# A graph network on one core: the attention targets' a_dst by a broadcast DMA from DRAM, and the gathered slots' lane at every pair of blocks

## The chip, the cores and the metric

The kernel runs on one core of a Trainium2 chip. The core has a matrix engine (TensorE; PE for its matmuls, PEld for the loads of its stationary operand), VectorE (DVE), ScalarE (ACT), GpSimd (POOL) and SyncE (SP), which here only issues DMAs. Sixteen DMA engines serve all queues. The metric is the device time of one execution in microseconds (us); less is better.

## The reference

Four graph layers follow each other over the same 6250 nodes with 128 features and the same 206250 edges, sorted by target. After each layer its result is added to x and normalised. The change touches the end of the third layer and the fourth, a graph attention with 4 heads of 32 channels:

```python
h = (x @ W).reshape(N, H, C)
a_src = jnp.sum(h * att_src, axis=-1)
a_dst = jnp.sum(h * att_dst, axis=-1)
logits = a_src[src] + a_dst[dst]
logits = jnp.where(logits > 0, logits, NEG_SLOPE * logits)
seg_max = jax.ops.segment_max(logits, dst, num_segments=N)
e = jnp.exp(logits - seg_max[dst])
denom = jax.ops.segment_sum(e, dst, num_segments=N)
alpha = e / (denom[dst] + EPS)
msgs = h[src] * alpha[:, :, None]
out = jax.ops.segment_sum(msgs, dst, num_segments=N)
```

So a_dst is one number for each node and head: 25000 numbers in all.

## The kernel before

Nodes lie in 49 blocks of 128, the last of 106. Layer 0 builds a dense adjacency (how often each source meets each target, in bf16) and stores it in DRAM as `adj`; layer 1 works on edges; layers 2 and 3 stream `adj` back. The program order is written out by hand: each engine, and SP's queue of DMAs, takes its instructions in that order.

**Layer 2 (`dense2`).** It goes over 25 targets' stretches of 256 nodes, two blocks each (below also called a block, counted from 0). `add(sb, ...)` first issues the loads of that stretch's adjacency on SP (L1061: four tiles of 11 source blocks, 704 KB each, and one of 5), then runs 3 x 49 matmuls (L822), and after every ten of them takes a step or two of `node2` for an earlier stretch. The first three stretches begin early, and up to stretch 6 two steps are taken each time, one afterwards. `A11` has six buffers, so the loads of the next stretch can start while this one is being summed. At a stretch's end ACT takes the sum out (L1078).

**`node2`** computes the new x, `h` and the attention terms: `al[:, 0]` holds a_src and `al[:, 1]` a_dst, one column for each block and head, with the node on the partition. For each of the two a product (L531) and a reduce (L533) run on DVE. Then two stores go out on SP (L537): h and a_src, into `t3`, which the gather of layer 3 reads. The loads of a later stretch stand behind those stores in SP's queue.

**Layer 3 (`attend`).** 48 target blocks are summed densely: six groups of 1024 targets times four heads give 24 units (counted from 0), each with 25 pairs of source blocks. For a pair, SP loads 512 KB of adjacency (L1390, four DMAs, three pairs ahead, four buffers), ACT makes a mask `r` from a_dst along the free axis and a_src as the bias (L1423, twice), DVE forms `B` and `C` (L1429, L1431), and PE runs ten matmuls of 512 columns (L1444). The pairs' loop ends with one step of each of four lanes:

- `sums`: `close` of the unit before, then `targets` of the next unit. A step is due two pairs after the last.
- `news`: the tables of the next head (ACT casts at L1239, DVE subtractions at L1241). The first head's tables are made inside unit 0.
- `ends`: the final normalisation of finished groups.
- `others`: `gathered`, the last block of 106 targets. It takes the block's sources by gathers on POOL (64 of 128 rows each), in eight chunks of eight slots: three adds on DVE, an exp on ACT (L1342), a product on DVE (L1345) and 16 matmuls into a sum on PE (L1348; each float32 product counts as two). Gathers run three chunks ahead, with four buffers.

**`targets`** brings a_dst of a unit's 1024 targets onto all partitions, as the free axis of a tile `ad`: for each of its eight blocks PE transposes the column of `al`, broadcast over 128 columns (L1259), into one PSUM bank, and ACT copies each four of them to SBUF (L1256, L1264).

Of the kernel before, what the change touches and what calls it, by code (L numbers as in the profile page):

```python
# [9 lines left out]
F32 = mybir.dt.float32  # L10
# [8 lines left out]
P = 128  # L19
# [4 lines left out]
F = 512  # L24
D = 128
HEADS = 4
# [42 lines left out]
def kernel(  # L69
# [9 lines left out]
    nc = tc.nc  # L79
    N = x.shape[0]  # L80
# [27 lines left out]
    dram = ctx.enter_context(tc.tile_pool(name="dram", bufs=1, space=bass.MemoryType.DRAM))  # L108
# [15 lines left out]
    R0 = rest[0][0] // P if rest else NB  # L124
    slot_src = dram.tile([max(2, 2 * NS - R0 // 2 * 2), P, S], I32)
    slot_not = dram.tile([max(2, 2 * NS - R0 // 2 * 2), P, S], F32)
    t3d = dram.tile([N + W, 2 * HEADS], F32)
    adj = dram.tile([NS, P, NB * 2 * P], BF16)
    ea_rows = edge_attr.rearrange("(r t) d -> r (t d)", t=T)

    def store(table, t, n0, rows, nb, eng=nc.sync):
        eng.dma_start(table[n0 : n0 + rows * nb].rearrange("(b p) d -> p b d", p=rows), t[:rows, :nb, :])
# [11 lines left out]
    ident = const.tile([P, P], F32)  # L144
# [201 lines left out]
    def transposed(pool, pps, t, rows, nb, name, G=4):  # L346

        pt = pps.tile([P, F], F32, name="na")
        for b in range(nb):
            nc.tensor.transpose(pt[:, b * rows : (b + 1) * rows], t[:rows, b, :], ident[:rows, :rows])  # L350
        yield
        r = pool.tile([P, G * P], F32, name=name)
        nc.scalar.copy(r[:, : rows * nb], pt[:, : rows * nb])
        yield
        return r
# [19 lines left out]
    def update(pool, po, n0, rows, nb, plus=None, G=4):  # L375

        xb = xn[:, n0 // P : n0 // P + nb, :]
        t = pool.tile([P, G, D], F32, name="res")
        nc.vector.tensor_add(t[:rows, :nb], po[:rows, :nb], (xb if plus is None else plus)[:rows, :nb])
        yield from layernorm(pool, t, xb, rows, nb)  # L380
        return xb
# [120 lines left out]
    def node2(acc, al, pool, pps, n0, rows, nb, G=4, hT=None):  # L502

        n = rows * nb
        b0 = n0 // P
        keep = hT is not None
        if not keep:
            hT = pool.tile([P, G * P], F32, name="hT")
            nc.scalar.activation(hT[:, :n], acc[:, 0, n0 : n0 + n], AF.Relu, bias=c1c)
        m = pool.tile([P, G, D], F32, name="m")  # L510
        nc.gpsimd.tensor_add(m[:rows, :nb], xn[:rows, b0 : b0 + nb, :], c2b[:rows].unsqueeze(1).to_broadcast([rows, nb, D]))
        yield
        po = pps.tile([P, 4, D], F32, name="na")
        for b in range(nb):
            nc.tensor.matmul(po[:rows, b, :], hT[:, b * rows : (b + 1) * rows], V2s, start=True, stop=True)
        yield
        xb = yield from update(pool, po, n0, rows, nb, m, G)
        xT = yield from transposed(pool, pps, xb, rows, nb, "xT", G)
        ph = pps.tile([P, 4, D], F32, name="na")
        for b in range(nb):  # L520
            nc.tensor.matmul(ph[:rows, b, :], xT[:, b * rows : (b + 1) * rows], Wgs, start=True, stop=True)
        yield
        if keep:
            hs = acc[:, 0, n0 : n0 + nb * D].rearrange("p (b d) -> p b d", d=D)
        else:
            hs = pool.tile([P, G, HW], F32, name="hs")
        nc.scalar.copy(hs[:rows, :nb, :D], ph[:rows, :nb])
        yield
        for k in range(2):
            pr = pool.tile([P, G, D], F32, name="pr")  # L530
            nc.vector.tensor_mul(pr[:rows, :nb], hs[:rows, :nb, :D],  # L531
                                 att[:rows, k : k + 1, :].to_broadcast([rows, nb, D]))
            nc.vector.tensor_reduce(al[:rows, k, b0 : b0 + nb, :],  # L533
                                    pr[:rows, :nb].rearrange("p b (h c) -> p b h c", h=HEADS), AX.X, ALU.add)
        if keep:
            for c, of in ((slice(0, D), hs), (slice(D, HW), al[:, 0, b0 : b0 + nb, :])):
                nc.sync.dma_start(t3[n0 : n0 + n, c].rearrange("(b p) d -> p b d", p=rows), of[:rows, :nb])  # L537
        else:
            nc.vector.tensor_copy(hs[:rows, :nb, D:], al[:rows, 0, b0 : b0 + nb, :])
            store(t3, hs, n0, rows, nb)  # L540
# [103 lines left out]
    def general():  # L644
        with ExitStack() as st:
# [113 lines left out]
            al = gp.tile([P, 2, NB, HEADS], F32, name="al")  # L759
            nc.vector.memset(al, 0.0)  # L760
            nodes("g2", lambda *a: node2(acc, al, *a))
            with tc.tile_pool(name="g3o", bufs=1) as one, tc.tile_pool(name="g3op", bufs=2, space=PSUM) as pps:
                drain(shift3(acc, al, one, one, pps))
# [4 lines left out]
    def fast():  # L768
# [401 lines left out]
        def attend(acc, al):  # L1170
# [9 lines left out]
            for k in range(2):  # L1180
                of = flat[:, k * US : (k + 1) * US].rearrange("p (n k c) -> p n k c", k=3, c=CH + 1)
                tabs.append((of[:, : 2 * NB].rearrange("p (b s) k c -> p b s k c", s=2), of[:, 2 * NB :]))
            units = [(groups[2 * k][0], groups[2 * k : 2 * k + 2]) for k in range(UNITS)]
            with tc.tile_pool(name="f3c", bufs=1) as one, tc.tile_pool(name="f3", bufs=2) as ep, \
# [62 lines left out]
                def width(of):  # L1247
                    return sum(rows * nb for n0, rows, nb in of)

                def targets(k, h, n0, of):  # L1250

                    to = one.tile([P, 2 * F], F32, name=f"ad{k % 2}")
                    last = None
                    for m0, rows, nb in of:
                        if last is not None:
                            nc.scalar.copy(*last)  # L1256
                        pt = pps.tile([P, F], F32, name="na")
                        for j in range(nb):
                            nc.tensor.transpose(pt[:, j * rows : (j + 1) * rows],  # L1259
                                                al[:rows, 1, m0 // P + j, h : h + 1].to_broadcast([rows, P]),  # L1260
                                                ident[:rows, :rows])
                        last = (to[:, m0 - n0 : m0 - n0 + rows * nb], pt[:, : rows * nb])
                        yield
                    nc.scalar.copy(*last)  # L1264
                    ready[k] = to

                def close(h, of, s):
# [122 lines left out]
                            nc.sync.dma_start(A[i][:, k, :n].rearrange("p l q -> p (l q)"),  # L1390
                                              adj[sb + k, :, a * 2 * P : (a + n) * 2 * P])

                sums, news, ends, others = Lane(), Lane(), Lane(), Lane(3)
                for i in range(3):
                    load(i)
                drain(targets(0, *steps[0]))
                first = [tables(0, groups[k::2]) for k in range(2)]
                others.add(gathered())
                made, i, now = 0, 0, 0
                for k, (h, n0, of) in enumerate(steps):  # L1400
# [6 lines left out]
                    if k + 1 < len(steps):  # L1407
                        sums.add(targets(k + 1, *steps[k + 1]))
# [49 lines left out]
        with tc.tile_pool(name="facc", bufs=1) as one:  # L1458
            acc = one.tile([P, 3, NA], F32, name="acc")
            for k in range(3):  # L1460
                nc.vector.memset(acc[:, k, :], 0.0)

            two, third = [acc[:, k, 0 : NB * D].bitcast(BF16).rearrange("p (b k d) -> p k b d", k=2, d=D) for k in (1, 2)]
            parts = [two[:, 0], two[:, 1], third[:, 0]]
            al = one.tile([P, 2, NB, HEADS], F32, name="al")
            nc.vector.memset(al, 0.0)
            with tc.tile_pool(name="f1n", bufs=1) as pool, tc.tile_pool(name="f1np", bufs=2, space=PSUM) as pps:
                left = mlp("f1", lambda *a: node1(acc, parts, *a), pool, pps)
                dense2(parts, lambda *a: node2(acc, al, *a), left)
            attend(acc, al)  # L1470
# [40 lines left out]
```

## Time and profile before

| | us |
|---|---|
| median of 18 runs (5471.37 to 5515.95) | 5495.12 |
| the profiled execution | 5501.77 |
| its span | 5500.0 |
| layer 2's last sum ends | 3888 |
| attention's pairs (first B to last) | 3910.7 to 5447 |
| PE busy, share of the span | 91% |
| DVE, ACT, POOL busy | 55%, 47%, 36% |

The profile is one execution. In the lines below a row of the timeline has start, duration, engine, line of the program, operation, output and inputs, a count, and in brackets the idle time before it with what ended it. "SPq" is SP's queue: the time is that of issuing, not of the transfer. In a row of stretches each engine has its busy time and number of instructions; a matmul's record is modelled, so neighbouring ones can overlap a little. PEclk is the clock granted to TensorE, 1.00 at most. Names of tensors are cut to letters: `t` is t3, `acc` here also holds h.

### The profile page before, as it was taken

To read this page: it belongs to the slowest core of one execution; us is meant where nothing else is said; L and a number is where in the kernel's file an instruction comes from. 1 tells how busy PE (TensorE), PEld (TensorE's weight loads), DVE (VectorE), ACT (ScalarE), POOL (GpSimd) and SP (SyncE) were. 2 spreads that over 40 slices of the span, in tenths; PEclk is the share of its full clock that TensorE was granted. 3 is DMA by queue.
4 is the path that set the end of the run, shared out by engine and by line. 5 is a ranking of instruction groups with operands and counts; after the bars stand their busy time and mean duration, and the time that the engine had idled before them with its cause. 6 is when DMAs were issued, how large, how long until landed. Compare 5 with 4: busy or idle time off the path is not lost.

```text
span 5500.0 us, 90840 instructions
## 1 busy us (share of the span) xinstructions
PE 4991.0 (91%) x33477; PEld 4101.3 (75%) x33477; DVE 3026.8 (55%) x5156; ACT 2569.3 (47%) x3618; POOL 1969.7 (36%) x1926
## 2 busy tenths in 40 slices
PE   4999997889899998998998999999689999999995
PEld 3999997788888887887888888899455555555553
DVE  6887863233333333332333333222578888888998
ACT  3444442222333332332332323100478999999885
POOL 3333425665666666656666566000220000000000
PEclk9999998998998998989998889999899999999998
DMA  5333324444444444444444443455476777777774
GB/s 115 120 134 130 144 108 136 126 124 123 128 127 127 127 130 122 127 120 126 123 126 124 118 123 109 169 196 196 144 176 193 220 215 211 221 215 218 211 212 125
DMA packets 624753, 830.17 MB, mean 151 GB/s; under 512 B 150523, under 2 KB 508449, under 8 KB 620077
## 3 DMA queue, kind: packets, MB, share of 16 engines
q1 hardware_dynamic: 536189, 595.08, 35.0%
q0 software_dynamic: 87120, 228.54, 14.6%
q8 instruction: 268, 4.39, 0.3%
q14 instruction: 184, 1.51, 0.1%
q10 hardware_dynamic: 992, 0.66, 0.0%
HBM read 730.60 MB, written 93.31 MB: 150 GB/s over the span
## 4 chain that ended last, share of the span: by engine, by line
PE 35%; ACT 7%; DVE 5%; DMA 2%; issue 2%; SPq 1%; another core or an unknown queue 1%; DVEq 0%; POOL 0%; ACTq 0%; POOLq 0%
PE s L1444 12%; PE sum L822 7%; PE seg L1143 6%; ACT r L1423 6%; PE pre L1129 5%; DVE B L1429 2%; DMA A<-adj 2%; PE na L1282 1%; PE tp L1118 1%; SPq L1390 1%; DVE sT L1275 0%; ACT acc L1239 0%; PE na L456 0%; DVE C L1431 0%
## 5 line engine op out<-in xcount | busy, mean ns | idle before, releaser
L135 POOL DMA_INDIRECT g<-t,edges x1617 | 1584.4, 980 | 1004.1 <-issue 762.8
L1423 ACT ACTIVATE r<-ad,bias 128x1024 bf16<-128x1024 f32 x1176 | 1254.1, 1139 | 107.0 <-DVE B L1429 104.7
L1131 DVE TENSOR_TENSOR g<-g,pre 128x512 f32<-128x512 f32 x882 | 548.7, 641 | 1304.9 <-PE pre L1129 416.6
L1444 PEld LDWEIGHTS <-acc 128*99 128x99 bf16 x5856 | 737.6, 127 | 663.9 <-issue 172.0
L1143 PE MATMUL seg<-oh,g 128*128 128x64 f32 (+1 forms) x6468 | 1036.6, 284 | 50.2 <-issue 47.2
L1143 PEld LDWEIGHTS seg<-oh,g 128*128 128x128 f32 (+1 forms) x6468 | 959.7, 205 | 93.0 <-issue 59.1
L1129 PE MATMUL pre<-W1s,eaT 128*128 128x256 f32 (+1 forms) x3234 | 908.0, 423 | 113.1 <-DVE g L1131 64.1
L1444 PE MATMUL s<-B,acc 128*99 128x512 bf16 x3504 | 874.6, 384 | 111.7 <-DVE B L1429 97.5
L1132 ACT ACTIVATE g<-g 128x512 f32<-128x512 f32 x882 | 505.8, 592 | 764.4 <-DVE g L1131 528.9
L1129 PEld LDWEIGHTS pre<-W1s,eaT 128*128 128x128 f32 (+1 forms) x3234 | 644.5, 212 | 246.7 <-issue 111.4
L1429 DVE TENSOR_TENSOR B<-A,r 128x2048 bf16<-128x2048 bf16 x600 | 720.6, 1201 | 137.2 <-ACT r L1423 71.3
L1120 ACT COPY eaT<-tp 128x512 f32<-128x512 f32 (+1 forms) x441 | 240.3, 545 | 1021.1 <-PE tp L1118 295.5
L1143 PE MATMUL seg<-oh,ea 128*128 128x64 f32 (+1 forms) x3234 | 664.2, 287 | 33.4 <-issue 33.0
L1143 PEld LDWEIGHTS seg<-oh,ea 128*128 128x128 f32 (+1 forms) x3234 | 526.6, 204 | 36.9 <-issue 36.8
L939 ACT CAST A<-pa 128x784 bf16<-128x784 f32 x400 | 324.4, 811 | 350.6 <-PE pa L936 323.3
L822 PE MATMUL sum<-A,xs 128*128 128x256 bf16 (+1 forms) x3675 | 471.0, 275 | 0.4 <-ACT A L939 0.4
L1431 DVE TENSOR_TENSOR C<-A,B 128x1024 bf16<-128x1024 bf16 x600 | 415.4, 692 | 68.0 <-PE s L1444 3.6
L822 PE MATMUL sum<-A,acc 128*128 128x256 bf16 (+1 forms) x3675 | 409.5, 271 | 4.4 <-DMA A<-adj 4.4
L822 PEld LDWEIGHTS <-acc 128*128 128x128 bf16 x3675 | 355.2, 98 | 46.2 <-issue 6.1
L822 PEld LDWEIGHTS <-xs 128*128 128x128 bf16 x3675 | 358.8, 102 | 36.8 <-issue 0.6
L936 PE MATMUL pa<-oh,oh 128*128 128x98 bf16 x3200 | 355.8, 268 | 26.9 <-ACT A L939 22.3
L1444 PE MATMUL s<-C,acc 128*99 128x512 bf16 x1200 | 360.2, 382 | 0.3 <-DVE C L1431 0.2
(242 smaller groups left out, 4099.7 us busy)
## 6 DMA issues: line engine op xcount, KB each, us to landing
A<-adj SPq DMA_DIRECT2D x2304, 128.0 KB
ea<-in_edge_attr_dram SPq DMA_DIRECT2D x292, 256.0 KB
A<-adj SPq DMA_DIRECT2D x100, 704.0 KB
ea<-in_edge_attr_dram SPq DMA_DIRECT2D x146, 192.0 KB
g<-t,edges POOLq DMA_INDIRECT x1617
A<-adj SPq DMA_DIRECT2D x25, 320.0 KB
t<-y SPq DMA_DIRECT2D x24, 256.0 KB
A<-adj SPq DMA_DIRECT2D x96, 64.0 KB
```

The lines of the kernel that those rows point to most:

```text
L135: nc.gpsimd.indirect_dma_start(out=to, out_offset=None, in_=table, in_offset=bass.IndirectOffsetOnAxis(ap=index[:K, t : t + 1], axis=0))
L822: nc.tensor.matmul(ps[:, :n], parts[part][:, b, :], a(b)[:, :n], start=k == 0, stop=k == 3 * NB - 1)
L936: nc.tensor.matmul(ps[:, o, q * LO : (q + 1) * LO], ohs[g][0][:, 2 * j + o, :, q], ohs[g][1][:, 2 * j + o, :, q], start=True, stop=True)
L939: nc.scalar.copy(A[sb][:, :, q0 : q0 + 2 * QI].rearrange("p k (o q) -> p k o q", q=QI), ps[:, :, : QI * LO].rearrange("p o (q k) -> p k o ...
L1129: nc.tensor.matmul(pre[:K, t, :], eaT[i][:, b + t, :K], W1s[:, 1, :], start=True, stop=True)
L1131: nc.vector.tensor_add(gb, gb, pre[:K, :n, :])
L1132: nc.scalar.activation(gb, gb, AF.Relu)
L1143: nc.tensor.matmul(ps[:, m, :], rows, oh[c][:K, a + t, :], start=a + t == 0 and m == 0, stop=a + t == T - 1, skip_group_check=True)
L1423: nc.scalar.activation(r[:, l, :n], ad[:, :n], AF.Relu, bias=bias[:, b + l, h : h + 1], scale=BIG)
L1429: nc.vector.tensor_tensor(wide(bt), At[:, :ns, :kk, :w], wide(r), ALU.min)
L1431: nc.vector.tensor_sub(ct[:, :n].rearrange("p (s q) -> p s q", q=w), At[:, :ns, 0, :w], bt[:, 0, :n].rearrange("p (s q) -> p s q", q=w))
L1444: nc.tensor.matmul(s[to][g][:M, : c1 - c0], row, rhs(c0, c1), start=to not in begun, stop=stop)
```

## The change

Layer 2 also writes a_dst to a DRAM tile with a row for each head: for each block one DMA from `al`, an element of 4 bytes for each node and head, issued on SP ahead of the two t3 stores. `targets` becomes one DMA on SP that reads 1024 numbers of a row and writes them to all 128 partitions; its transposes and copies go. It has one step in the `sums` lane where it had three. And `others` is due at every pair where it was due at every third.

```diff
+    a_dst = dram.tile([HEADS, N], F32)
...
         if keep:
+            with nc.allow_non_contiguous_dma(reason="one element a node and head"):
+                for b in range(nb):
+                    nc.sync.dma_start(a_dst[:, n0 + b * rows : n0 + (b + 1) * rows].rearrange("h p -> p h"),
+                                      al[:rows, 1, b0 + b, :])
             for c, of in ((slice(0, D), hs), (slice(D, HW), al[:, 0, b0 : b0 + nb, :])):
...
                     to = one.tile([P, 2 * F], F32, name=f"ad{k % 2}")
-                    last = None
-                    for m0, rows, nb in of:
-                        if last is not None:
-                            nc.scalar.copy(*last)
-                        pt = pps.tile([P, F], F32, name="na")
-                        for j in range(nb):
-                            nc.tensor.transpose(pt[:, j * rows : (j + 1) * rows],
-                                                al[:rows, 1, m0 // P + j, h : h + 1].to_broadcast([rows, P]),
-                                                ident[:rows, :rows])
-                        last = (to[:, m0 - n0 : m0 - n0 + rows * nb], pt[:, : rows * nb])
-                        yield
-                    nc.scalar.copy(*last)
+                    nc.sync.dma_start(to[:, : width(of)], a_dst[h, n0 : n0 + width(of)].partition_broadcast(P))
+                    yield
                     ready[k] = to
...
-                sums, news, ends, others = Lane(), Lane(), Lane(), Lane(3)
+                sums, news, ends, others = Lane(), Lane(), Lane(), Lane(1)
```

## The prediction

> **What bounds the kernel now.** I read the busy time of each engine in stretches first, the timeline of one block of layer 2 next, then the waits of the attention stage and the transfers' packets.
>
> Busy times by stretch (span, then PE, PEld, DVE, ACT, POOL in us with counts, granted clock, DMA share, GB/s): a block of layer 2, then, from a second answer, attention units 0, 1, 2, then 5 to 18, then 19 to 22.
>
> ```profile
> 3724.00:3741.00 17.00, 17.00 (x158) 15.36 (x156) 3.59 (x12) 1.35 (x5) 0.72 (x1) 1.00 0.53 191
> ```
> ```profile
> 3910.70:4010.00 99.30, 71.08 (x270) 39.55 (x271) 61.50 (x106) 65.91 (x84) 37.39 (x34) 0.81 0.49 139
> 4010.00:4084.30 74.30, 63.55 (x316) 39.43 (x316) 57.12 (x85) 57.83 (x65) 19.58 (x19) 0.98 0.78 188
> 4084.30:4163.50 79.20, 68.43 (x315) 41.16 (x315) 56.71 (x83) 56.16 (x62) 9.79 (x9) 0.89 0.71 174
> ...
> 4290.90:5124.60 833.70, 810.61 (x3976) 490.11 (x3974) 729.16 (x970) 772.79 (x823) 0.00 (x0) 1.00 0.72 217
> 5124.60:5377.80 253.20, 233.95 (x1141) 140.54 (x1140) 237.40 (x407) 221.29 (x230) 0.00 (x0) 1.00 0.70 211
> ```
> Layer 2 is PE without a gap. A steady attention unit lasts 833.7/14 = 59.6 us, with PE busy 57.9 and ACT 55.2. Units 19 to 22 lean on DVE too (94%). Units 0 to 2 are 15 to 40 us longer, and PE is not what fills them.
>
> How little lead layer 2 has, from its timeline (start, us, engine, line): block 15 first, then the end of block 3.
>
> ```profile
> 3733.99 0.37 SPq L537 DMA_DIRECT2D t<-acc  x1
> ...
> 3734.91 0.37 SPq L537 DMA_DIRECT2D t<-al  x1
> ...
> 3735.37 2.87 SPq L1061 DMA_DIRECT2D A<-adj  x5
> 3735.37 0.42 DVE L533 TENSOR_REDUCE al<-pr 128x8 f32<-128x256 f32 x1
> 3740.91 0.47 ACT L1078 ACTIVATE hT<-sum,c1c 128x256 f32<-128x256 f32 x1 [6.94 <-PE sum L822]
> ```
> ```profile
> 3528.88 2.71 SPq L1061 DMA_DIRECT2D A<-adj  x5
> ...
> 3532.28 0.47 ACT L1078 ACTIVATE hT<-sum,c1c 128x256 f32<-128x256 f32 x1 [4.76 <-PE sum L822]
> 3533.54 1.25 PE L822 MATMUL sum<-A,acc 128*128 128x256 bf16 x10 [1.29 <-DMA A<-adj]
> ```
> The loads of the next block stand on SP behind the stores of this one's node work. At block 4 they left at 3528.88 and PE began on them at 3533.54: 4.66 us from issue to use, and PE stood 1.29 us. In a steady block they leave 3735.37 and are wanted when the sum before is done, 3740.91 (less 0.03): a lead of 5.51. The slack is 0.85 us. By the packets' own times the first tile lands 1.57 us before that end on average, which gives 0.6. I take 0.7.
>
> Waits of the attention stage (who, on whom: us, times, longest), units 4 to 18, then units 1 and 2; and the transfers during one gather:
>
> ```profile
> DVE B L1429 <- ACT r L1423: 49.3, 53, 2.2
> ...
> ACT ad L1256 <- PE na L1259: 29.5, 15, 2.1
> ```
> ```profile
> DVE B L1429 <- DMA A<-adj: 25.5, 11, 3.7
> ```
> ```profile
> q1 hardware_dynamic: 4171, 3.80, 53.5%
> q0 software_dynamic: 256, 0.54, 33.1%
> ```
> ACT stands about 2 us in each unit for the transposes that carry a_dst. In units 1 and 2 the wait for adjacency tiles is 25.5 us, and in the 24 us window over one chunk of slots the gather (q0) holds a third of the DMA engines.
>
> **The change, part by part.**
>
> *Transposes and copies go.* Per unit 8 transposes (four take 0.43 us on PE, from 4497.63 to the next matmul at 4498.06: 0.87 a unit) and two ACT copies (14.03 + 13.81 us in 24 units: 1.16 a unit), with the 2 us wait ahead of the first. What that is worth depends on who bounds. PE alone gives 0.87 a unit. PE has 833.7 - 810.6 = 23 us idle in 14 units, 1.65 each, so a unit can give 2.5 at most. I take 1.3 for units 3 to 18 (PE-bound ones give 0.87, those in which the next head's tables are made and ACT is full give more), 21 us; 0.9 in the other seven, 6 us; and 1 us of copies ahead of the first r. Sum -28; bounds -14 (DVE-bound and early units give nothing) and -48.
>
> *A broadcast of 512 KB a unit comes.* 24 DMAs on SP, each 128 packets of 4 KB. Packets of 4096 bytes took 0.16 us in stage 1, so 1.3 us of all 16 engines, at pair 9 of 25, right behind a load and ahead of the next. Steady tiles land 1 to 2.5 us before B needs them, so the next load is late by about 1 us and nothing stands; the target row is wanted 15 pairs later. On SP the issue is 0.43 us where four loads of 0.43 fill 1.9 of a pair's 2.4 us. I take +2; bounds 0 and +12 (0.5 us a unit).
>
> *The first broadcast* waits for all of layer 2's a_dst writes and stands behind 12 tile loads on SP (3893.8 to 3899.4); landed about 3905, before the first r at 3908.5, which waits for tables. Zero; if the last block's 424 writes are slow, +3.
>
> *Stores of a_dst come into layer 2.* 49 DMAs of 512 elements of 4 bytes, two for each pair of blocks, ahead of the t3 stores and waiting for the second reduce of al, which ends at 3735.79. Today the t3 stores fit into the wait for DVE; then they queue behind it. SP's order is then: 3735.82 two stores at 0.46 (512-element stores of the output issue in 0.37 to 0.43), then two t3 stores at 0.46, then the loads at 3737.66: 2.3 us later than 3735.37. DVE, ACT and PE get no new work; what is queued behind SP is only the loads, and PE waits for those. Less the slack, 2.3 - 0.7 = 1.6 us a block for blocks 8 to 24 (17 blocks, all with the same lead to 0.6 us): 27 us. Block 4 has no slack: 2.3. Blocks 5 to 7 have 9.9 us of lead: nothing. Sum +29.5.
>
> The price of 4-byte writes into DRAM is in no row. The nearest is the t3<-al store, 16 bytes each: one DMA's 256 packets, in a window that also holds 16 others:
>
> ```profile
> DMA packets 272, 0.00 MB, mean 7 GB/s; under 512 B 272, under 2 KB 272, under 8 KB 272
> ```
> It fits into 0.23 us, so 512 would take 0.46, no longer than SP needs to issue one, and nothing is added. Four times that (3.7 us for two) would put the loads behind a backlog and the delay at 4.75: +70 us in all. Bounds for the part +20 (slack 0.85 and issues of 0.37) and +70; I stay with the row, which is the same queue, store and place.
>
> [...]
>
> *The lane of the gathered slots steps at every pair, not every third.* Chunks 4 to 7 of the gather now start at pairs 24, 36, 48 and 60 (POOL at 4002, 4038, 4073, 4114) and would start at 14, 18, 22 and 26. So three fall into unit 0, where B needs a tile 5 to 7 us after it lands (packet times; in units 1 and 2 it is 1 to 4). Three quarters of the 25.5 us go: -19. PE's sums (16 matmuls, 1.8 us a chunk): five chunks leave units 2 to 4, three come into unit 1, two go into unit 0's idle PE: -3.5. Unit 0 gets two more chunks of DVE work (1.22 + 3 x 0.19 = 1.8 each): +3.6. ACT's exp now comes one pair after DVE's adds (0.57 us) and can stand about 0.5 each, eight times: +4. On POOL a chunk's eight gathers take 10 us (1.25 each) where four pairs of unit 0 last 16, so the data, wanted 12 pairs after its issue, is not late, and POOL has nothing else queued; the two slot loads on SP stay where they are. Sum -15; bounds -26 (every wait gone, no cost) and +8 (waits only moved).
>
> **Sum:** 29.5 - 28 - 15 + 2 = -11.5 us. The profiled execution took 5501.8 us (span 5500.0), 6.7 above the median of 5495.1. Set against the median: 5484.
>
> **The rivals.** *Layer 2 pays more* (ends slower). The 4-byte writes drain slower than 16-byte ones, or SP takes 0.97 us to issue one, as it did for the 550 single elements at the start. [...] Against: the 16-byte row. Each microsecond of delay costs 18 us, so it is even at 2.9 us and slower by 0.2% from 3.5; at 4 us the time is 5495 - 11.5 + 31 = 5515. *The lane moves its waits, not ends them:* for it, that gathers 0 to 3 already cost unit 0 waits; against it, unit 0's spare lead. Part +4 in place of -15: 5503. *The delay in layer 2 is hidden*, because landing and use overlap better than block 4 shows: two blocks that landed 1.03 us ahead ran on within 0.06 us. Then -41: 5454.
>
> The clock gate: PE's 1.29 us wait at block 4 left the granted clock at 1.00. [...]
>
> **How the numbers follow.** The sum as worked 0.45 (alone 5462 to 5507: about half faster by over 0.2%, a third within); layer 2 pays more 0.30 (nearly all slower); the lane's waits stay 0.13 (half slower, half within); hidden 0.12 (faster). 0.2%, 11 us, is what a measurement here can tell. Faster 0.37, within 0.20, slower 0.43. Cases of both signs weigh alike, so the range goes from the hidden case to beyond the first rival's 4 us: 5452 to 5525.
>
> **What would show it.** PE sum waiting for the adjacency DMA in layer 2, about 18 times for some 30 us, with blocks of 18.8 us in place of 17.2. SP's loads 2.3 us later against the end of the sum. The 29.5 us wait of ACT gone, and steady units of 58.3. Units 1 and 2 together 15 to 20 us shorter, unit 0 up to 8 longer. Wrong if layer 2's wait is 60 us or none, or if B comes to wait for tiles at pair 12 or 13 of each unit.

## The result

The changed kernel takes 5917.73 us (median of 10 runs, 5912.39 to 5930.81) where the kernel before takes 5493.25 (median of 62): 1.0774 times as long, 95% interval 1.0757 to 1.0791, or 424 us more. The forecast was 5484 us with a range of 5452 to 5525. It missed by far: the time lies 393 us above the range.

### The profile page after: what moved, and what is told of

It is laid out like the page before. It is cut to its first block, busy times and chain, and to the rows that moved or that the text cites. A ratio compares the mean times of both kernels' runs of the same rounds, so it can differ in the third digit from the quotient of the medians.

```text
span 5879.9 us, 90525 instructions
## 1 busy us (share of the span) xinstructions
PE 4977.1 (85%) x33285; PEld 4076.5 (69%) x33285; DVE 3017.6 (51%) x5156; ACT 2549.2 (43%) x3570; POOL 1969.2 (33%) x1926
## 5 line engine op out<-in xcount | busy, mean ns | idle before, releaser
L1148 PE MATMUL seg<-oh,g 128*128 128x64 f32 (+1 forms) x6468 | 1031.1, 283 | 40.3 <-issue 37.4
L827 PE MATMUL sum<-A,acc 128*128 128x256 bf16 (+1 forms) x3675 | 451.2, 286 | 379.1 <-DMA A<-adj 379.1
L827 PEld LDWEIGHTS <-acc 128*128 128x128 bf16 x3675 | 374.5, 104 | 442.0 <-issue 384.3
L380 DVE TENSOR_TENSOR res<-na,m 128x256 f32<-128x256 f32 (+2 forms) x63 | 29.4, 467 | 656.1 <-PE na L516 595.6
```

Of the source, the lines that this page charges most:

```text
L827: nc.tensor.matmul(ps[:, :n], parts[part][:, b, :], a(b)[:, :n], start=k == 0, stop=k == 3 * NB - 1)
L1148: nc.tensor.matmul(ps[:, m, :], rows, oh[c][:K, a + t, :], start=a + t == 0 and m == 0, stop=a + t == T - 1, skip_group_check=True)
```

## The profile after

The profiled execution of the changed kernel took 5881.72 us with a span of 5879.9, 36 us below its median. The page of after, first: PE's busy tenths, POOL's and the clock granted to PE in 40 slices of 147 us; then the group of layer 2's matmuls, from the page of before and from that of after (busy time and mean ns; the idle time ahead of them, and what ended it).

```profile
PE   4999989899989888999998985555558999999995
...
POOL 3333326666666665566666610000040000000000
PEclk9999988999999998898988997777779999999998
```
```profile
L822 PE MATMUL sum<-A,acc 128*128 128x256 bf16 (+1 forms) x3675 | 409.5, 271 | 4.4 <-DMA A<-adj 4.4
```
```profile
L827 PE MATMUL sum<-A,acc 128*128 128x256 bf16 (+1 forms) x3675 | 451.2, 286 | 379.1 <-DMA A<-adj 379.1
```

Six slices, 880 us, have PE half idle and its clock at 0.7: they are layer 2 (POOL, which gathers in the stages on both sides, is idle there). Its matmuls wait 379.1 us for adjacency tiles where they waited 4.4, and are themselves busy 451.2 us where 409.5 were: the same 3675 matmuls, at a granted clock of 0.77 over layer 2 where it was 1.00.

One block of layer 2 and the start of the next, from the timeline after (start, duration, engine and line; SPq rows are times of issue):

```profile
3720.29 0.42 DVE L534 TENSOR_REDUCE al<-pr 128x8 f32<-128x256 f32 x1
3720.74 0.92 SPq L539 DMA_DIRECT2D a_dst<-al  x2
3721.75 0.46 SPq L542 DMA_DIRECT2D t<-acc  x1
3722.26 0.46 SPq L542 DMA_DIRECT2D t<-al  x1
3722.81 9.99 SPq L1066 DMA_DIRECT2D A<-adj  x5
3725.83 0.47 ACT L1083 ACTIVATE hT<-sum,c1c 128x256 f32<-128x256 f32 x1 [6.94 <-PE sum L827]
3743.92 4.26 PE L827 MATMUL sum<-A,acc 128*128 128x256 bf16 x20 [18.13 <-DMA A<-adj]
...
3758.11 0.92 SPq L539 DMA_DIRECT2D a_dst<-al  x2
```

SP's order is the one that was forecast: two stores at 0.46, two at 0.46, then the loads, which leave 3.02 us before ACT begins to take out the sum (5.54 in the kernel before). But the first tile's data lands some 20 us after its issue, not 4, and PE stands 18.13 us. A block lasts 37.4 us (3720.74 to 3758.11) where one lasted 17.2.

What the transfers did in the stretch from the loads' issue to PE's start (3722.8 to 3743.9, 40 slices of 0.53 us; the DMA row is the busy share of the engines, GB/s what they moved):

```profile
DMA  9733627999756991999590099009056136796989
GB/s 191 2 1 2 4 2 29 45 90 35 12 2 22 65 32 0 22 43 53 21 32 0 21 53 43 0 0 53 0 32 43 43 64 85 107 171 160 267 246 342
DMA packets 744, 1.28 MB, mean 61 GB/s; under 512 B 305, under 2 KB 538, under 8 KB 744
```

And SP's own waits in one period (3722 to 3758.5; who, on whom, us, times, longest):

```profile
SPq L539 <- DVE al L534: 16.5, 1, 16.5
SPq L539 <- DMA a_dst<-al: 8.7, 1, 8.7
SPq L1066 <- DMA a_dst<-al: 4.5, 1, 4.5
SPq L1066 <- PE sum L827: 2.0, 1, 2.0
```

After the first half microsecond the engines are held most of the time and move 0 to 90 GB/s for some 17 us, and only then 85 to 342. In the trace SP's DMAs carry eight semaphores in turn (100 and 102 to 108), and a landing is recorded as updates of the one its DMA carries: from 3576 to 4280 each of 173 DMAs has 16 of them before SP issues the DMA eight after it, and 18 times that one goes out within 0.1 us of the last. So these waits tell when the a_dst stores were complete. The fifth load, issued at 3732.48, waited 4.5 us for the first store, whose issue had ended at 3721.1 and whose last update came at 3732.46: 11.4 us. The next block's store waited 8.7 us, from 3732.8 to 3741.5, for the second, whose issue had ended at 3721.7: 19.9 us. 1024 elements of 4 bytes take about 20 us to complete, 20 ns each. Yet in the packet records nothing of this shows at the stores themselves: 1056 packets of 4 bytes (the 1024 elements and 32 more) start and end within 1 us, with records of 7 to 9 ns, like those of the 16-byte row that priced them. What is long are records of packets behind them: tile packets of 5632 bytes, 0.2 us as a rule, take 1.7 to 9.0 us in the slowest tenth of layer 2's.

Where the 380 us between the two profiled executions (5501.8 and 5881.7) lie:

| stretch | before | after | difference |
|---|---|---|---|
| layer 2, third sum's end to last sum's | 375.5 | 791.5 | +416 |
| last sum's end to attention's first B | 22.7 | 38.1 | +15 |
| attention, first B's start to last B's end | 1528.8 | 1500.2 | -29 |
| everything up to the third sum's end | 3512.5 | 3489.5 | -23 |

(In the profile of before the last B ends at 5439.5, not at 5447.) Layer 2's 416 are the wait and the clock: 379.1 - 4.4 = 374.7 of waiting, 451.2 - 409.5 = 41.7 of slower matmuls, together 416.4.

The +15 at the attention's start is the last block's backlog. SP's rows after, from the timeline:

```profile
4287.10 0.27 SPq L539 DMA_DIRECT2D a_dst<-al  x1
4287.47 12.48 SPq L542 DMA_DIRECT2D t<-acc  x1
4299.99 0.65 SPq L542 DMA_DIRECT2D t<-al  x1
4300.74 10.03 SPq L1385 DMA_DIRECT2D A<-adj  x12
4310.82 0.43 SPq L1258 DMA_DIRECT2D ad<-a_dst  x1
```

The first `r` waits for that broadcast until 4316.9.

Attention units 0, 1 and 2, then 5 to 18, then 19 to 22 (span, PE, PEld, DVE, ACT and POOL busy, clock, DMA share, GB/s):

```profile
4319.20:4412.50 93.30, 69.37 (x304) 41.83 (x305) 66.10 (x115) 64.69 (x83) 60.61 (x54) 0.86 0.69 159
4412.50:4496.70 84.20, 68.24 (x349) 43.39 (x348) 62.41 (x103) 56.72 (x66) 11.84 (x11) 0.94 0.76 176
4496.70:4557.50 60.80, 55.98 (x273) 33.65 (x272) 53.96 (x82) 55.23 (x63) 0.00 (x0) 1.00 0.72 218
...
4676.50:5503.50 827.00, 796.30 (x3866) 478.19 (x3865) 724.31 (x970) 761.16 (x795) 0.00 (x0) 1.00 0.76 227
5503.50:5757.70 254.20, 232.71 (x1109) 137.47 (x1108) 237.12 (x407) 218.37 (x222) 0.00 (x0) 0.99 0.73 218
```

Units 0 to 2 are 14.5 us shorter in sum (238.3 against 252.8), and a steady unit lasts 59.07 us in place of 59.55. PE's and ACT's work fell by about 1 us a unit, as forecast; half of that did not become time.

## The experiments

The chips differ: the kernel before takes 5484 us (5455.75 to 5504.88) on the chip of `stores_only`, `lane_only`, `rows` and `rows_lane3`, and 4984 on the two chips of the other eight, whose PE is granted a higher clock in the earlier stages (in `lane_only` 0.90 from 860 to 2900 us, in `late_rows` 0.99 over the same work, 860 to 2500). So times are compared on one chip, or as ratios.

**Is the whole loss the stores?** `stores_only` is the kernel before with the change's stores in layer 2; nothing reads them, and attention is as it was. `lane_only` is the other end: the lane alone.

```diff
+    a_dst = dram.tile([HEADS, N], F32)
...
         if keep:
+            with nc.allow_non_contiguous_dma(reason="one element a node and head"):
+                for b in range(nb):
+                    nc.sync.dma_start(a_dst[:, n0 + b * rows : n0 + (b + 1) * rows].rearrange("h p -> p h"), al[:rows, 1, b0 + b, :])
```

> The kernel before with the 49 a_dst stores added and nothing else (nothing reads them). If the loss is the 4-byte writes: blocks of layer 2 go from 17.2 to about 37 us as in the changed kernel, the time is 5900 to 5950 us, PE waits some 380 us for adjacency tiles in layer 2, and attention after its first pairs is as before (steady units 59.6 us). If the broadcasts or the lane made the loss, or part of it, the time stays within 100 us of before.

Measured: 5920.56 us, ratio 1.0797 (1.0759 to 1.0836), 436 us more than before's 5484.06. Layer 2 takes 794.2 us, 37.6 a block. So the stores alone make the whole loss, and the attention's part of the change gives a little back.

**What makes a store cost 20 us?** Five variants of `stores_only`, one execution each, all against the 4984 us of before on the faster chips. Their tables are written and not read; `stores_one_head` stores one head's quarter.

```diff
 stores_pitch64
+    a_dst = dram.tile([HEADS, N, 16], F32)
+                    nc.sync.dma_start(a_dst[:, n0 + b * rows : n0 + (b + 1) * rows, 0].rearrange("h p -> p h"), al[:rows, 1, b0 + b, :])
 stores_pitch512
+    a_dst = dram.tile([HEADS, N, 128], F32)
 stores_16B
+    a_dst = dram.tile([N, HEADS], F32)
+                    nc.sync.dma_start(a_dst[n0 + b * rows : n0 + (b + 1) * rows, :], al[:rows, 1, b0 + b, :])
 stores_one_head
+                    nc.sync.dma_start(a_dst[0:1, n0 + b * rows : n0 + (b + 1) * rows].rearrange("h p -> p h"), al[:rows, 1, b0 + b, 0:1])
 stores_act
+                    nc.scalar.dma_start(a_dst[:, n0 + b * rows : n0 + (b + 1) * rows].rearrange("h p -> p h"), al[:rows, 1, b0 + b, :])
```

> The kernel before with the same 49 stores of 512 elements of 4 bytes, each element now 64 bytes from the next in DRAM; nothing reads them. If the writes are slow because neighbours in one memory line come from several DMA engines at once: the backlog goes and a block of layer 2 lasts 18.8 us (the 2.3 us of SP's order less the slack), 5520 to 5530 us. If a write of 4 bytes is slow wherever it goes: 37 us a block and about 5900, as with the stores of the change.

> The kernel before with the 4-byte stores 512 bytes apart. At 64 bytes a block of layer 2 lasted 20.5 us, 1.7 above what SP's order alone gives (18.8). If sharing a larger line or row than 64 bytes still costs: 18.8 us a block here. If the rest is the price of any 4-byte write: 20.5 again.

> The kernel before with a_dst stored as 16 bytes a node, side by side ([N, 4]): the same bytes in a quarter of the writes, four nodes to 64 bytes. If the number of writes into shared lines counts, at the 20 us for 1024 writes that the changed kernel shows, 256 writes add 5 us: blocks of 23 to 24 us, about 5640. If 16 bytes are cheap as in the t3 store: 18.8 us a block, 5520 to 5530.

> The kernel before with the a_dst stores of one head of four: 256 writes of 4 bytes a block, 128 contiguous words each. If the cost goes by the number of writes: 5 us and SP's 1.6, blocks of 23 to 24 us, about 5640. If the four heads collide with each other and one does not: 18.8 us.

> The kernel before with the a_dst stores issued by ACT on its own queue instead of SP. If the loads only stand behind the writes in SP's queue: they leave as before and blocks stay at 17.2 to 17.7 us, about 5495. If the writes pile up in memory and hold the DMA engines whatever queue they came from: loads are late by nearly as much, blocks of 30 us and over.

Measured, with three rows of comparison (from chips of the slower kind) first. "Block" is the mean time of one; "lands" is the median time from the loads' issue to the end of the first tile's last packet, "SP" that from the start of the first load's issue to the start of the fifth's, "wait" PE's wait for tiles in layer 2, "busy" that of its matmuls:

| | packets a block | us over before | block | lands | SP | wait | busy |
|---|---|---|---|---|---|---|---|
| before | none | 0 | 17.2 | 3.9 | 2.1 | 4.4 | 409.5 |
| stores_only | 1024 of 4 B, side by side | +436 | 37.6 | | | 372.7 | 455.4 |
| after | the same | +424 | 37.5 | 20.1 | 9.9 | 379.1 | 451.2 |
| stores_pitch64 | 1024 of 4 B, 64 B apart | +68 | 20.6 | 4.6 | 2.4 | 51.3 | 425.6 |
| stores_pitch512 | 1024 of 4 B, 512 B apart | +55 | 20.4 | 4.5 | | 48.3 | 426.5 |
| stores_16B | 256 of 16 B, side by side | +72 | 20.8 | 5.1 | | 54.8 | 425.7 |
| stores_one_head | 256 of 4 B, side by side | +202 | 27.6 | 10.7 | 6.8 | 170.8 | 447.5 |
| stores_act | 1024 of 4 B, side by side, ACT's queue | +136 | 22.7 | 5.5 | 4.0 | 109.5 | 438.1 |

Number and size of the packets are the same in `stores_only` and `stores_pitch64`; only the addresses differ, and the first tile lands after 4.6 us in place of 20. At 512 bytes apart it is no better than at 64. A quarter of the packets side by side is far dearer than all of them apart. So what costs is neither the count of packets nor, by itself, their size of 4 bytes: it is writing neighbouring 4-byte elements of one stretch of DRAM. With the 16-byte elements side by side the tile lands nearly as soon as with those spread out; these are as many packets as in `stores_one_head`, on the same chip. The semaphores tell it of the stores themselves: a block's second store is complete 20.0 us (median) after the end of its issue in `after`, 1.6 in `stores_pitch64` and `stores_pitch512`, 1.4 in `stores_16B`, and 8.4 in `stores_one_head`, so that 256 neighbours cost more than a quarter of what 1024 do.

In `stores_pitch64` the timeline shows what the forecast had meant to price:

```profile
3347.88 0.92 SPq L539 DMA_DIRECT2D a_dst<-al  x2
3348.91 0.44 SPq L541 DMA_DIRECT2D t<-acc  x1
3349.68 0.36 SPq L541 DMA_DIRECT2D t<-al  x1
3350.14 2.92 SPq L1065 DMA_DIRECT2D A<-adj  x5
3352.97 0.47 ACT L1082 ACTIVATE hT<-sum,c1c 128x256 f32<-128x256 f32 x1 [6.94 <-PE sum L826]
3355.33 2.34 PE L826 MATMUL sum<-A,acc 128*128 128x256 bf16 x20 [2.40 <-DMA A<-adj]
```

and a window of layer 2 (165 us; after the clock come the DMA share and GB/s) what such stalls do to the clock:

```profile
3205.00:3370.00 165.00, 144.39 (x1242) 126.24 (x1240) 28.70 (x96) 12.10 (x32) 5.80 (x8) 0.95 0.48 162
```

Even stores that are complete after 1.6 us cost 47 us of waiting and 16 of slower matmuls: 63, twice the 29.5 that the forecast took.

On ACT's queue the stores no longer stand ahead of the loads, but they still slow them: SP needs 4.0 us for the five loads, and the wait is 109.5 us in 35 pieces, the longest 16.1. So it is only partly the order within one queue; the rest is held up in what the queues share. Part of that is the semaphores: in the trace ACT's DMAs take theirs from the same eight as SP's, and SP's loads in layer 2 waited 37.0 us, in twelve pieces, for an a_dst store that ACT had issued. The transfers are slowed too: a t3 store of h, complete 1.5 us after its issue in `rows`, takes 6.2 (medians). Whether that is the DMA engines or the memory itself, these runs don't tell, nor how far apart neighbours must lie (64 bytes apart they add 68 us, 512 apart 55, and 16-byte elements side by side 72).

**What is the attention part worth without those stores?** `rows` writes the same table another way: PE transposes a_dst to four rows, ACT copies them and sends rows of 1024 bytes on its own queue. `rows_lane3` is `rows` with the lane of before, Lane(3).

```diff
 rows, in node2, in place of the change's stores
+            yield
+            pa = pps.tile([P, F], F32, name="na")
+            for b in range(nb):
+                nc.tensor.transpose(pa[:HEADS, b * rows : (b + 1) * rows], al[:rows, 1, b0 + b, :], ident[:rows, :rows])
+            yield
+            adT = pool.tile([HEADS, G * P], F32, name="adT")
+            nc.scalar.copy(adT[:, :n], pa[:HEADS, :n])
+            nc.scalar.dma_start(a_dst[:, n0 : n0 + n], adT[:, :n])
...
 lane_only
-                sums, news, ends, others = Lane(), Lane(), Lane(), Lane(3)
+                sums, news, ends, others = Lane(), Lane(), Lane(), Lane(1)
```

> The changed kernel, but a_dst reaches DRAM in rows: two steps after the t3 stores PE transposes the columns of al (4 targets' rows, 256 columns), ACT copies them and issues the store, 1 KB a row, on its own queue. If the loss is the 4-byte writes and nothing else: blocks of layer 2 are back at 17.2 to 17.5 us, and the time is before plus what attention gains in the changed kernel's trace (units together 32 us shorter): 5450 to 5475 us. If any added store at that place delays the loads, blocks stay above 18.5 us and the time is over 5500.

> As the run with rows, but the gathered lane again at every third pair. If the lane is worth 15 to 20 us as units 0 to 4 suggest (23 us shorter together in the changed kernel), this is 15 to 23 us above the run with rows, 5470 to 5490. If the lane only moves waits, both are equal within 5 us and the gain is the targets' alone.

> The kernel before with the gathered lane at every pair and nothing else. If the lane's gain is its own: 5470 to 5480 us, units 2 to 4 shorter by about 27 us together, units 0 and 1 longer by about 4. If it moves waits only: 5490 to 5500.

Measured: `rows` 5474.75, ratio 0.9985 (0.9956 to 1.0013); `rows_lane3` 5492.51, 1.0011 (0.9979 to 1.0044); `lane_only` 5482.94, 0.9995 (0.9962 to 1.0028). None is told from no change by its time; the stages in the profiles tell more:

| | layer 2 | units 0 to 4 | a unit of 5 to 18 | first B to last end |
|---|---|---|---|---|
| before | 375.5 | 380.3 | 59.55 | 1528.8 |
| lane_only | 376.0 | 369.7 | 59.59 | 1519.4 |
| rows_lane3 | 385.5 | 376.4 | 59.39 | 1521.2 |
| rows | 386.8 | 362.0 | 59.22 | 1507.2 |

The lane gives 10.6 us alone and 14.4 beside the new `targets` (units 0 to 4; one execution each, and `stores_only`, with attention as before, has 382.1 there). It does so as was argued, by moving gathers forward. Units 0, 1 and 2 of `lane_only` against 99.3, 74.3 and 79.2 of before:

```profile
3905.10:4008.90 103.80, 73.36 (x316) 43.39 (x317) 66.27 (x115) 66.28 (x87) 57.60 (x51) 0.84 0.63 143
4008.90:4094.00 85.10, 68.86 (x352) 43.90 (x352) 62.58 (x102) 57.37 (x67) 10.97 (x10) 0.92 0.73 166
4094.00:4154.80 60.80, 57.56 (x284) 34.78 (x282) 54.38 (x83) 56.10 (x65) 0.00 (x0) 1.00 0.71 212
```

Units 0 and 1 take more of the gathers' work and become longer, unit 2 loses 18 us, and units 3 and 4 are free of it (60.4 and 59.6 us for 64.4 and 63.1).

`targets` by broadcast, though, gives a steady unit 0.2 to 0.3 us, not 1.3. The timeline of `rows` around one broadcast shows where the rest goes:

```profile
4529.92 0.38 SPq L1262 DMA_DIRECT2D ad<-a_dst  x1
...
4536.95 1.22 DVE L1428 TENSOR_TENSOR B<-A,r 128x2048 bf16<-128x2048 bf16 x1 [2.83 <-DMA A<-adj]
4538.22 1.46 PE L1443 MATMUL s<-B,acc 128*99 128x512 bf16 x6 [1.11 <-DVE B L1428]
```

Seven microseconds behind it DVE stands 2.83 us for a tile, and PE stands 1.11 behind DVE. In the whole of units 5 to 18 of before B waited for tiles four times, 2.3 us in all, in the changed kernel twenty times (before, then after):

```profile
DVE B L1429 <- DMA A<-adj: 2.3, 4, 1.4
```
```profile
DVE B L1424 <- DMA A<-adj: 21.9, 20, 3.3
```

In layer 2 `rows` pays 11.3 us for its added steps (386.8 against 375.5), which takes half of what the attention gains.

**Which queue should the broadcast take?** `late_rows` leaves layer 2 as it was. It turns all of a_dst by two transposes at the attention's start, copies it on ACT and sends it from there. Then `late_rows` broadcasts on SP, as the change does, `late_rows_pool` on POOL's queue, `late_rows_act` on ACT's. All three have the change's lane.

```diff
+    a_dst = dram.tile([HEADS, NB * P], F32)
...
+                cols = one.tile([P, NB, HEADS], F32, name="neg").rearrange("p b h -> p (b h)")
+                nc.vector.tensor_copy(cols.rearrange("p (h b) -> p h b", h=HEADS), al[:, 1].rearrange("p b h -> p h b"))
+                turned = one.tile([P, 2 * F], F32, name="ad1")
+                a_rows = a_dst.rearrange("h (b p) -> (h b) p", p=P)
+                pt = pps.tile([P, F], F32, name="na")
+                for k in range(0, HEADS * NB, P):
+                    m = min(P, HEADS * NB - k)
+                    nc.tensor.transpose(pt[:m, k : k + P], cols[:, k : k + m], ident)
+                for k in range(0, HEADS * NB, P):
+                    m = min(P, HEADS * NB - k)
+                    nc.scalar.copy(turned[:m, k : k + P], pt[:m, k : k + P])
+                    nc.scalar.dma_start(a_rows[k : k + m], turned[:m, k : k + P])
...
 late_rows_act (late_rows_pool: nc.gpsimd.dma_start)
-                    nc.sync.dma_start(to[:, : width(of)], a_dst[h, n0 : n0 + width(of)].partition_broadcast(P))
+                    nc.scalar.dma_start(to[:, : width(of)], a_dst[h, n0 : n0 + width(of)].partition_broadcast(P))
```

> The changed kernel without any a_dst store in layer 2: attention's start puts all of a_dst into a head-major tile (one DVE copy), turns it with two PE transposes, copies it on ACT and stores it in 196 rows of 512 bytes on ACT's queue; broadcasts on SP and the lane at every pair as in the change. Layer 2 is that of before (17.2 us a block), the broadcasts land before the first r, attention is 20 to 30 us shorter than before: ratio to before 0.995 to 0.996. If the first broadcast is late, the first B comes up to 6 us later.

> As the run with late rows, with the broadcasts issued by POOL. If the adjacency tiles come late behind a broadcast because it stands ahead of them in SP's queue and holds one of its eight semaphores: B's wait for tiles in units 5 to 18 falls from 30 us to under 10 and steady units drop from 59.2 to about 58.3, 15 to 20 us less in all. If it is the transfer's own 1.3 to 1.7 us of all engines: no change within 5 us.

> As the run with late rows, with the broadcasts issued by ACT's hardware queue. Same two readings as with POOL; ACT pays 0.4 us of issue a unit, so at best 1 us a unit is won against SP, about 10 us less than the run on SP. If only the engines' time counts: equal to SP within 5 us.

| broadcast on | median us | ratio to before (interval) | a unit of 5 to 18 | first B to last end |
|---|---|---|---|---|
| SP | 4967.42 | 0.9971 (0.996 to 0.9982) | 59.17 | 1498.2 |
| POOL | 4991.68 | 1.0014 (1.0005 to 1.0023) | 60.27 | 1518.9 |
| ACT | 4948.06 | 0.9937 (0.9923 to 0.995) | 58.04 | 1477.2 |

The last column is not to be set against the 1528.8 of before, which is of a slower chip: `stores_pitch512`, with attention as before and on the chip of these three, has 1516.4 (its unit 0 lasts 88.7 us for 99.3, its steady units 59.58). So attention changes by -18, +3 and -39 us. Layer 2 is back at 17.16 us a block, and the first B comes 24.3 us after the last sum, 1.6 later than before. Units 5 to 18 of the three, waits that differ (`late_rows`, then `late_rows_pool`, then `late_rows_act`):

```profile
DVE B L1432 <- DMA A<-adj: 30.0, 31, 3.1
...
SPq L1393 <- DMA ad<-a_dst: 15.1, 13, 2.1
```
```profile
DVE B L1432 <- DMA A<-adj: 52.2, 39, 4.0
...
SPq L1393 <- DMA A<-adj: 19.1, 16, 2.2
```
```profile
DVE B L1432 <- DMA A<-adj: 19.1, 31, 1.5
```

With the broadcast on SP, a load waits about 1.2 us in nearly every unit (13 times in 14) for the broadcast to be complete: the eight semaphores again, and tiles come late to B. From ACT's queue SP no longer waits for it, B's longest wait halves to 1.5 us, and a steady unit is 58.04 us, 1.5 below before. `late_rows_act` is the best version: 36 us, 0.63%, below the kernel before on the same chip. On POOL B waits more, not less as was expected; its transfers hold the loads up (SP waits 19.1 us for earlier loads, 0.5 in `late_rows`), and by what is shown only in part.

The three runs differ not only in the queue but in when the broadcast leaves. In units 5 to 18 SP issues it 27 to 28 us into a unit, ACT 18 to 21, POOL, as soon as the tile `ad` is free, 3 to 7 us before the next unit begins. It is complete 4 to 6 us after its issue on each. ACT's takes one of SP's eight semaphores too, but the load that needs it next comes 7.4 to 8.0 us after the issue, when the broadcast is complete; on SP that load waits, and goes out 4.2 to 5.9 us after it. POOL's DMAs carry semaphores of their own (111 to 118 in the trace of the changed kernel), and there 30 of B's 52.2 us of waiting come at the first two pairs of a unit, just behind the broadcast. So whether ACT's queue helps, or only the earlier issue, these runs don't separate.

## Why the prediction was wrong, step by step

**The price of the a_dst stores failed: "It fits into 0.23 us, so 512 would take 0.46, no longer than SP needs to issue one, and nothing is added."** Measured, 512 such elements complete after 11 us and 1024 after 20. The row that priced them was of 256 packets of 16 bytes, 528 bytes apart in `t3`; it had neither the size nor the neighbouring addresses of the new ones, and it gave the time of packets in the engines, not that until the write is complete and the next transfer gets through. The size was in view: that 4-byte writes "drain slower than 16-byte ones" stood among the rivals, but no row of before had a store of adjacent small elements whose completion could be read, and the bound of four times the row was no bound of an unseen kind of access. The term was +29.5 with bounds +20 and +70; it measured +416 in layer 2. Slower had the largest of the forecast's chances, 0.43, but at prices that ended at 5525.

Size alone is not the reason in these runs: 1024 packets of 4 bytes spread 64 bytes apart add 0.7 us to the tile's landing (4.6 against 3.9), side by side 16.2 (20.1). And the end of a store's packets was not its completion: they ended within 1 us, where the waits for stores issued on SP show 11 and 20.

**The first rival was right in kind and far too small.** "Layer 2 pays more" had the mechanism, and 4 us of delay as its price. What came was 18 us a block. Its sentence "each microsecond of delay costs 18 us" holds: 18 us a block for 20 blocks is the wait's 375.

**The delay of the loads was about right, the slack of 0.7 us was not there.** 2.3 us later was forecast, and 2.5 measured (lead 5.54 to 3.02). `stores_pitch64` measures this step by itself: 2.5 us of PE's wait a block in 19 blocks, where 1.6 was worked out; issue to use is 5.2 us there, not 4.66, and the first tile lands 0.7 us later than in before. The clock was the other part missed: one stall of 1.29 us had left it at 1.00, but stalls of 2.5 us every 20 give 0.95, and 18 us give 0.77 over layer 2. In `stores_pitch64` a stall of 2.57 us, up to 3166.7, was followed by 3.4 us at a clock of 0.50, one of 2.29 us, up to 3146.8, by none.

**The first broadcast, "Zero; if the last block's 424 writes are slow, +3", was wrong by the same step:** +15, as SP could issue the last t3 store only in 12.5 us and the twelve loads in 10.

**The lane was right in size.** -15 was forecast; -10.6 to -14.4 came. B's waits for tiles in units 1 and 2 fell from 25.5 to 10.7 us in `lane_only` (-19 was forecast; in the six runs with nothing but stores added they are 15.4 to 26.0), and unit 0 became 4.5 us longer (up to 8). The gain lay partly elsewhere than said: units 1 and 2 together give 7.6 us, not 15 to 20, and units 3 and 4 give 7.5. The rival that its waits only move doesn't fit these stages; the whole times can't tell.

**The targets' gain could be had, and the broadcast's cost was wrong.** "Steady tiles land 1 to 2.5 us before B needs them, so the next load is late by about 1 us and nothing stands." B stood: its waits for tiles in units 5 to 18 went from 2.3 us to 21.9. Both signs that the forecast named as proof of an error showed: layer 2's wait far over 60 us, and B waiting for tiles at pairs 12 and 13 of a unit (18.5 of the 21.9 us). SP's waiting for a DMA eight places earlier was not in the working at all. So of 1.3 us a unit 0.2 to 0.5 remained, and with the broadcast off SP's queue the unit gave 1.5. The attention's part of the forecast was -28 - 15 + 2 = -41; with layer 2 as before and the broadcast on ACT's queue the whole kernel gains 36.

## What to carry to other kernels

A store that scatters 4-byte elements side by side into DRAM cost 20 ns an element here (1024 of them) for whatever was queued behind it, though its own packets look quick; transpose on chip and store rows (11 us more in layer 2 here), or give each element 64 bytes (63 more). Read a store's price from when a DMA that waits for it, or stands behind it, gets through, and when no row has its size and address pattern, do not let a smaller price from another pattern close the range. The wait for a semaphore eight DMAs back is part of the cost of a half-megabyte broadcast among prefetch loads, about 1.2 us a unit here: let it leave so early that it is complete when the load that takes its semaphore comes, as from ACT's queue here, and look at what stands behind it, as POOL's queue shows.

## What was unexpected of the hardware

- 256 neighbouring 4-byte writes a block cost more (+202 us) than 1024 at 64 bytes apart (+68), and 64 bytes were as good as 512.
- Stores on ACT's queue slowed loads on SP's: the five loads took 4.0 us to issue in place of 2.1, and both queues take the same eight semaphores.
- Writes whose packets ended within 1 us held back reads for 17 us: the tiles behind them moved at 0 to 90 GB/s, then at up to 342.
- Moving one broadcast a unit from SP's queue to ACT's, where it left some 9 us earlier in the unit, gave 19 us over the kernel, and to POOL's cost 24.
